# The last attention of an eight-layer kernel: its projections in pairs through a PSUM bank of their own

## The chip, the cores and the metric

The kernel runs on one core of a Trainium2 chip. The metric is the device time of one execution in microseconds; the runs shown are whole executions, and the profile is one further execution with the hardware profiler on.

## What is computed

Eight sequences of 256 tokens with 256 features pass through four layers, each an attention and a feed-forward part, both with a residual and a layer norm. All of it is in fp32. The change touches the last attention and, by one line, the mixture of experts behind it. Of the reference, what matters is this:

```python
# attention of layer 3: 16 heads of 16, 4 key heads, two score maps a = 0, 1 for each head
q, k = rope(x @ Wq), rope(x @ Wk)                       # 2 * 16 per head
scores = softmax(where(causal, NEG, q_a . k_a) / 4)     # for a = 0 and 1
lam = exp(sum(lq1 * lk1)) - exp(sum(lq2 * lk2)) + LAM_INIT
diff = softmax(where(causal, NEG, scores[0] - lam * scores[1]))
att = diff @ v
att = att * rsqrt(mean(att * att) + 1e-8) * rms_w * (1 - LAM_INIT)
x = layernorm(x + att @ Wo)
# feed-forward of layer 3: 32 experts, the 4 likeliest for each token
w, i = top_k(softmax(x @ gate), 4);  w = w / sum(w)
x = layernorm(x + sum_k w_k * down_i(up_i(x) * silu(gate_i(x))))
```

## The kernel before

The eight phases run one after the other (`attn0`, `ffn0`, ... `attn3`, `ffn3`). In `attn3` and `ffn3` the order of the instructions on PE, DVE, ACT and POOL is the order in which the program writes them; SP, which issues the DMAs, is ordered by a scheduler. [...]

`attn3` cuts a sequence into six units: two with the first 128 queries and two of four heads each (`qc` 0), and four with the last 128 queries, one head each (`qc` 1). The 48 units run as a pipeline of 51 rounds (loop at L833). In a round, for the unit n, PE multiplies queries and keys (L641) and adds the mask (L654), DVE takes four maxima (L658), ACT the exponentials with their sums (L661; 16 short ones for `qc` 0, 8 long ones for `qc` 1). For the unit n-1, `factors` (L667) prepares the ratio c on POOL, and `differences` (L686) takes the second map off the first on DVE in two halves (L695, L699), which POOL shifts and scales (L703). For n-2, `turned` (L709) transposes on PE and ACT takes the second exponential (L722). For n-3, `values` (L728) multiplies with V.

Beside this run two chains of small steps. `project(b)` (L584) makes the rotated queries and keys of the next sequence: 12 products of 128x256, each taken out of PSUM by DVE with a table (L599), and the product for V (L615, L619). The loop advances it by one step after `values` and by one or two after the first half of the differences. `finish(b)` (L748) ends a sequence. Its six steps are: (1) transpose the outputs, divide, square (L755 to L767); (2) root of the mean of squares (L770 to L789), for which ACT loads the table of Ln and then that of Exp (L779, L780) between POOL's small instructions, all in 32 columns; (3) transpose again and copy (L794, L798); (4) output product, residual, statistics (L803 to L808); (5) normalise; (6) transpose x for the next phase. The loop takes one step a round, after the first half. When sequence 3 has ended, the sort of the experts' group 0 begins as a third chain (`others`), whose last part scatters the rows by 32 indirect DMAs on POOL (L953), three a round.

PSUM has eight banks, two for each of four tags. The scores use `a` and `s`; `values` uses `o`; everything else uses `t`: the projections, `turned`, and steps 1, 3, 4 and 6 of `finish`.

`ffn3` (L2063) computes two groups of 63 tiles of 128 sorted rows. For each tile: fetch (L1959, three tiles in one DMA on SP), transpose (L1970), gate and up (L1978), Silu, transpose back (L1994), down (L2000, eight tiles later in the first group), copy to `yg` (L2008, two buffers) and store (L2010). Between the tiles of group 0, it works off what the attention left over: the last `finish`, and behind it the sort of group 1, whose scatter must have landed before group 1 is fetched:

```python
left = list(left) + [self.ffn3_sort(w, 1, act)]
for j, _ in enumerate(self.ffn3_experts(w, 0, act)):
    if len(left) > 1 and j % 3 != 2:
        continue
    while left and next(left[0], StopIteration) is StopIteration:
        left.pop(0)
```

Of the kernel before, what the change touches and what calls it, by code (L numbers as in the profile page):

```python
# [10 lines left out]
F32 = mybir.dt.float32  # L11
BF16 = mybir.dt.bfloat16
I32 = mybir.dt.int32
U32 = mybir.dt.uint32
AF = mybir.ActivationFunctionType
ALU = mybir.AluOpType
AX = mybir.AxisListType

P = 128
NB = 8  # L20
T = 256
D = 256
BLK = 512
NBLK = NB * T // BLK
LN_EPS = 1e-5
NEG = -1e30
# [5 lines left out]
TILES0 = [(n * T * 2 + 4 * (P - 1)) // P for _, n in GROUPS0]  # L32
ROW0 = P + 8
# [6 lines left out]
class Model:  # L40
# [493 lines left out]
    def attn3_load(self, pool, keep):  # L534
        wo = self.load(keep, "a3_wo", [P, 2, D])
        rms = self.load(keep, "a3_rms_w", [P, 1])
        l = pool.tile([P, 4, 256], F32, name="w_l", tag="w_l")
        for i, x in enumerate(("lq1", "lk1", "lq2", "lk2")):
            self.nc.sync.dma_start(out=l[:, i, :], in_=self.ins[f"a3_{x}"].to_broadcast([P, 256]))
        return dict(  # L540
            l=l,
            wq=self.load(pool, "a3_wq", [P, 2, 1024], split=2),
            wk=self.load(pool, "a3_wk", [P, 2, 512]),
            wv=self.load(pool, "a3_wv", [P, 2, 64]),
            wo=wo,
            tq=self.load(pool, "c_tq3", [P, 2, T]),
            ck=self.load(pool, "c_ck3", [P, 2, T]),
            sk=self.load(pool, "c_sk3", [P, 2, T]),
            rms=rms,
        )  # L550

    def attn3(self, w, act, keep, start=False, beside=None):
# [5 lines left out]
        nc = self.nc  # L558
        lam_init = 0.8 - 0.6 * math.exp(-0.3 * 0)

        e = []
        l = w["l"]
        for i in range(2):
            pr = l[:, 2 * i, :]
            nc.vector.tensor_tensor(pr, pr, l[:, 2 * i + 1, :], ALU.mult)
            sm = act.tile([P, 16], F32, tag=f"lsm{i}", name="lsm", bufs=1)
# [3 lines left out]
        nlam = act.tile([P, 4, 4], F32, tag="nlam", name="nlam", bufs=1)  # L570
        nl = nlam.rearrange("p s h -> p (s h)")
# [3 lines left out]
        wo = w["wo"]  # L575
        nc.vector.tensor_scalar(wo, wo, w["rms"], 1.0 - lam_init, ALU.mult, ALU.mult)
        Vs = []
        for i in range(2):
            V = act.tile([P, 2, 4, 32], F32, tag=f"V{i}", name=f"V{i}", bufs=1)
            nc.gpsimd.memset(V, 1.0)  # L580
            Vs.append(V)
        qTs, kTs, oT, oSs = {}, {}, {}, {}

        def project(b):  # L584

            if start:
                self.transpose_x(b)
            xT = self.xT[b // 2][:, :, (b % 2) * T : (b % 2 + 1) * T]
            qT = act.tile([P, 8, T], F32, tag="qT", name="qT")
            kT = act.tile([P, 2, T], F32, tag="kT", name="kT")  # L590

            def turn(out, wt, i, tab):
                ps = self.ps("t")[:, :T]
                for c in range(2):
                    nc.tensor.matmul(
                        ps, wt[:, c, i * P : (i + 1) * P], xT[:, c, :],
                        start=(c == 0), stop=(c == 1),
                    )
                nc.vector.tensor_tensor(out, ps, tab, ALU.mult)  # L599

            for a in range(2):
                k = kT[:, a, :]
                turn(k, w["wk"], 2 * a, w["ck"][:, a, :])
                yield
                x = act.tile([P, T], F32, tag="kh", name="kh", bufs=1)
                turn(x, w["wk"], 2 * a + 1, w["sk"][:, a, :])
                nc.gpsimd.tensor_tensor(k, k, x, ALU.add)
                yield
            for j in range(8):
                turn(qT[:, j, :], w["wq"], j, w["tq"][:, j % 2, :])  # L610
                yield
            ps = self.ps("t")[:, :128].rearrange("p (t n) -> p t n", t=2)
            for t in range(2):
                for c in range(2):
                    nc.tensor.matmul(  # L615
                        ps[:, t, :], xT[:, c, t * P : (t + 1) * P], w["wv"][:, c, :],
                        start=(c == 0), stop=(c == 1),
                    )
            nc.vector.tensor_copy(  # L619
                Vs[b % 2][:, :, :, 0:16], ps.rearrange("p t (s d) -> p t s d", s=4)  # L620
            )
            qTs[b], kTs[b] = qT, kT
            yield

        class Unit:

# [101 lines left out]
            def values(u):  # L728

                V = Vs[u.b % 2]  # L730
                if u.h0 == 0:
                    oT[u.b, u.qc] = self.ps("o").rearrange("p (h q) -> p h q", h=4)
                o = oT[u.b, u.qc]
                for c in range(1 + u.qc):
                    for s in range(4):
                        out = o[32 * s : 32 * s + 32, u.h0 : u.h0 + u.nh, :]
                        x = u.p[s] if u.qc == 0 else u.p[s][:, c : c + 1, :]
                        nc.tensor.matmul(
                            out, V[:, c, s, :], x, start=(c == 0), stop=(c == u.qc)
                        )  # L740
                if u.h0 + u.nh == 4:
                    oS = keep.tile([P, 4, P], F32, tag=f"oS{u.qc}", name="oS", bufs=1)
                    self.copy(oS, o)
                    oSs[u.b, u.qc] = oS
                    if u.qc == 1:
                        done.append(finish(u.b))
# [68 lines left out]
            yield  # L815

        others = []
        projections, ends, done = [], [], []

        def step(queue, n=1):  # L820

            while n and queue:
                if next(queue[0], StopIteration) is StopIteration:
                    queue.pop(0)
                else:
                    n -= 1

        for _ in project(0):
            pass
        units = [  # L830
            Unit(b, qc, h0) for b in range(NB) for qc in range(2) for h0 in range(0, 4, 2 - qc)
        ]
        for n in range(len(units) + 3):  # L833

            def at(back):
                return units[n - back] if 0 <= n - back < len(units) else None

            u, last = at(0), at(1)
            if u and u.qc == 0 and u.h0 == 0:
                step(projections, 100)  # L840
                if u.b + 1 < NB:
                    projections.append(project(u.b + 1))
            if last:
                last.factors()
            step(others)
            if u:
                u.scores()
            if at(3):
                at(3).values()
            step(projections)  # L850
            halves = last.differences() if last else iter(())
            next(halves, None)
            step(projections, 2 if u and u.qc == 0 else 1)
            step(ends)
            next(halves, None)
            next(halves, None)
            if not self.scattering:
                step(others, 2)
            if at(2):
                at(2).turned()  # L860
            ends += done
            done.clear()
        return ends + others
# [1199 lines left out]
    def ffn3(self, w, act, left, start=False):  # L2063

        self.down = None
        if start:
            for b in range(NB):
                self.transpose_x(b)  # L2070
            left = [self.ffn3_sort(w, 0, act)]
        if 0 not in self.sorted:
            for x in left:
                for _ in x:
                    pass
            left = []
        left = list(left) + [self.ffn3_sort(w, 1, act)]
        for j, _ in enumerate(self.ffn3_experts(w, 0, act)):

            if len(left) > 1 and j % 3 != 2:  # L2080
                continue
            while left and next(left[0], StopIteration) is StopIteration:
                left.pop(0)
        for x in left:
            for _ in x:
                pass
        put = self.ffn3_combine(0, act, 2)
        for j, _ in enumerate(self.ffn3_experts(w, 1, act)):

            if j >= 8:  # L2090
                next(put, None)
        for _ in put:
            pass
        for _ in self.ffn3_combine(1, act, 1):
            pass
# [194 lines left out]
```

## Time and profile before

| What | us |
|---|---|
| median of 3 runs | 2521.76 (2521.01 to 2522.95) |
| the profiled execution | 2531.46 |
| its span, first to last instruction | 2529.7 |
| opening projection, PE busy all the time | 1756 to 1768 |
| first scores of the attention | 1768.5 |
| attention, last differences begin | 2215.7 |
| first tile of the experts transposed | 2230.12 |
| last tile of group 0, first of group 1 | 2355.43, 2367.07 |
| combining the last outputs, to the end | 2473.9 to 2529.7 |

Over the whole span PE is busy 87%, DVE 57%, ACT 41%, POOL 36%, with a mean granted clock of 0.947 on PE. These shares are means over phases with different limits: in the attention it is DVE that has the least idle time. In the rows of the profile, a line such as L599 is the program's line, `out<-in` its tiles, and the text in brackets the idle time of the engine just before and what ended it. In the rows of waits the three numbers are the total in us, the number of times, and the longest. fp32 products show two matmul records for each instruction of the program.

### The profile page before, as it was taken

What the parts mean: (1) busy time and instruction counts of PE and PEld (TensorE: products, weight loads), DVE (VectorE), ACT (ScalarE), POOL (GpSimd) and SP (SyncE); (2) the same over time, 40 slices, a digit from 0 to 9 for tenths busy, and PEclk for the clock granted to TensorE, in tenths of its full rate; (3) what the DMA queues carried; (4) which work ended last, traced back from release to release, by engine and by line L of the source; (5) the groups of instructions that cost most, each with busy time, mean ns of one, the idle gap of its engine ahead of it and who ended that gap; (6) DMA issues with size and microseconds to landing.
All of it is one profiled execution on the core that took longest, in us unless ns stands there. A gap on an engine that the chain in (4) does not pass through costs nothing. (4 is left out here: it accounts for less than half of the span.)

```text
span 2529.7 us, 36310 instructions
## 1 busy us (share of the span) xinstructions
PE 2207.9 (87%) x12016; PEld 1497.5 (59%) x12016; DVE 1431.1 (57%) x3593; ACT 1046.2 (41%) x3005; POOL 917.4 (36%) x1725
## 2 busy tenths in 40 slices
PE   7999789899999999999999999998878777678990
PEld 4454588756666666666664465555555554467780
DVE  4555486754544544544465454565888888645363
ACT  1334355553544544534431112121766755634440
POOL 1222443343433323333312321000566647824445
PEclk9999999999999999999999999999989988789995
DMA  5000411100000100000250011002000000155663
GB/s 159 1 1 1 157 48 40 53 14 4 4 3 3 52 1 1 1 1 1 81 197 0 1 50 51 1 0 102 1 2 1 1 1 28 38 139 174 200 203 96
DMA packets 92309, 120.76 MB, mean 48 GB/s; under 512 B 9757, under 2 KB 79582, under 8 KB 91102
## 3 DMA queue, kind: packets, MB, share of 16 engines
q1 hardware_dynamic: 82270, 95.75, 11.8%
q0 software_dynamic: 8192, 21.11, 2.8%
q8 instruction: 100, 1.64, 0.3%
q10 hardware_dynamic: 1664, 1.57, 0.2%
q14 instruction: 83, 0.68, 0.1%
HBM read 67.53 MB, written 50.88 MB: 47 GB/s over the span
## 5 line engine op out<-in xcount | busy, mean ns | idle before, releaser
L1388 POOL TENSOR_SCALAR p<-p,rs 128x128 f32<-128x128 f32 (+1 forms) x256 | 104.6, 428 | 293.7 <-DVE rs L1386 289.4
L1378 ACT ACTIVATE p<-ps_s,nm,rq 128x128 f32<-128x128 f32 (+1 forms) x256 | 128.0, 507 | 151.0 <-DVE nm L1376 151.0
L1306 ACT ACTIVATE sq<-ps_a 128x512 f32<-128x512 f32 x126 | 76.0, 603 | 228.1 <-PE ps_a L1298 225.9
L146 POOL TENSOR_SCALAR rsq<-bnmv 128x2 f32<-128x2 f32 x64 | 13.6, 213 | 385.4 <-DVE bnmv L184 377.8
L661 ACT ACTIVATE e<-ps_a,nm 128x128 f32<-128x128 f32 (+1 forms) x256 | 105.9, 435 | 108.9 <-DVE nm L658 95.4
L1307 DVE TENSOR_REDUCE ssk<-sq 128x4 f32<-128x512 f32 x64 | 43.8, 686 | 172.6 <-ACT sq L1306 172.6
L703 POOL TENSOR_SCALAR v<-e,r,nmd 128x128 f32<-128x128 f32 (+1 forms) x256 | 134.9, 540 | 10.0
L1298 PE MATMUL ps_a<-w_a_wq,xT 128*128 128x512 f32 x256 | 123.2, 604 | 12.1 <-DVE k L1320 9.2
L1978 PE MATMUL ps_a<-w_f_gup,xTg 128*128 x504 | 113.1, 349 | 12.8 <-DVE xTg L1972 5.5
L720 PE MATMUL ps_t<-ident,v 128*128 128x128 f32 x384 | 67.8, 312 | 62.3 <-DVE qT L599 30.6
L1298 PE MATMUL ps_a<-w_a_wv,xT 128*128 128x512 f32 x256 | 120.5, 593 | 1.0 <-ACT q L1331 1.0
L695 DVE SCALAR_TENSOR_TENSOR e<-e,c 128x128 f32<-128x128 f32 (+1 forms) x256 | 105.6, 462 | 23.0 <-POOL c L682 22.8
L1307 DVE TENSOR_REDUCE ssq<-sq 128x4 f32<-128x512 f32 x64 | 43.9, 686 | 131.0 <-ACT sq L1306 131.0
L1298 PE MATMUL ps_a<-w_a_wk,xT 128*128 128x512 f32 x248 | 116.5, 593 | 0.0
L1426 PE MATMUL ps_o<-w_a_wo,attT 128*128 128x256 f32 x512 | 111.8, 379 | 0.0
L661 ACT ACTIVATE e<-ps_s,nm 128x128 f32<-128x128 f32 (+1 forms) x256 | 106.8, 451 | 0.0
L1426 PEld LDWEIGHTS ps_o<-w_a_wo,attT 128*128 128x128 f32 x512 | 96.7, 190 | 12.8
L1162 DVE SCALAR_TENSOR_TENSOR yg<-ps_t,xg,yg 128x128 f32<-128x128 f32 x266 | 93.1, 350 | 13.8 <-PE ps_t L1151 3.5
L1365 PE MATMUL ps_s<-kT,qT 128*128 128x256 f32 (+1 forms) x512 | 99.5, 327 | 0.0
L1978 PEld LDWEIGHTS ps_a<-w_f_gup,xTg 128*128 128x128 f32 x504 | 83.3, 199 | 25.2 <-issue 10.5
L720 PEld LDWEIGHTS ps_t<-ident,v 128*128 128x128 f32 x384 | 49.4, 160 | 81.8 <-POOL nmd L700 29.9
L1412 PE MATMUL ps_o<-pT,V 128*128 128x256 f32 x256 | 79.5, 392 | 19.3 <-ACT pT L120 19.3
(410 smaller groups left out, 6072.7 us busy)
## 6 DMA issues: line engine op xcount, KB each, us to landing
rows<-zero SPq DMA_DIRECT2D x42, 384.0 KB
xg<-rows SPq DMA_DIRECT2D x42, 384.0 KB
outs<-yg SPq DMA_DIRECT2D x42, 384.0 KB
w_f_gup<-in_f_gup SPq DMA_DIRECT2D x8, 768.0 KB
w_f_w<-in_f_w SPq DMA_DIRECT2D x8, 512.0 KB
w_f_down<-in_f_down SPq DMA_DIRECT2D x8, 384.0 KB
w_f_up<-in_f_up SPq DMA_DIRECT2D x5, 512.0 KB
lrows<-zero SPq DMA_DIRECT2D x12, 204.0 KB
```

The costliest lines, as they stand in the source:

```text
L661: nc.scalar.activation(e[:, s, j * nk : (j + 1) * nk], sc[s][:, j, :], AF.Exp, bias=nm[:, s, j : j + 1], scale=1.0, accum_out=sums[:, s, j ...
L695: nc.vector.scalar_tensor_tensor(d[:, s, h, :], u.e[:, s, h, 1, :], u.c[:, s, h : h + 1], d[:, s, h, :], ALU.mult, ALU.add,)
L703: nc.gpsimd.tensor_scalar(u.v[:, s, h, :], d[:, s, h, :], u.r[:, s, h, 0:1], nm[:, s, h : h + 1], ALU.mult, ALU.add,)
L720: nc.tensor.transpose(ps[:, s, c, :], x, self.ident)
L1162: nc.vector.scalar_tensor_tensor(acc[j], y, c, acc[j], ALU.mult, ALU.add)
L1298: nc.tensor.matmul(ps, self.xt(u.b, t, c), w[which][:, c, u.cols], start=(c == 0), stop=(c == 1),)
L1307: nc.vector.tensor_reduce(out, sq, AX.X, ALU.add)
L1365: nc.tensor.matmul(sc[:, j, :], u.qT[:, h0 + j, qc * P : (qc + 1) * P], u.kT[:, h0 + j, 0:nk], start=(j == 0), stop=False,)
L1378: nc.scalar.activation(u.p[qc][:, h0 + j, :], sc[:, j, :], AF.Exp, bias=nm[:, j : j + 1], scale=r[:, j : j + 1], accum_out=u.sums[qc][:, h ...
L1388: nc.gpsimd.tensor_scalar(u.p[qc][:, j, :], u.p[qc][:, j, :], ri[:, j : j + 1], 1.0, ALU.mult, ALU.mult,)
L1426: nc.tensor.matmul(y[:, t, :], attTs[b][:, h, t * P : (t + 1) * P], w["wo"][:, h, :], start=(h == 0), stop=(h == 15),)
L1978: nc.tensor.matmul(ps, xT[j][:, c, :], w["gup"][:, bass.ds(er[j], 1), c, :].rearrange("p o f -> p (o f)"), start=(c == 0), stop=(c == 1),)
```

## The change

`project(b)` no longer yields. It returns six pairs of a PE part and a DVE part, and a seventh for V. A pair makes two products side by side in one bank (128x512), which DVE takes out with one instruction. Keys are added on POOL with one instruction for both. One of the two `o` banks, `bank_x`, is kept for these pairs for the whole attention, and the other, `bank_o`, for `values`. In the loop, the PE part of a pair ends a round and its DVE part comes early in the next; V goes into the third round of a sequence. Before the loop, the six pairs and V of the first sequence run one after the other. `finish` gets two steps in each round.

```diff
-        qTs, kTs, oT, oSs = {}, {}, {}, {}
+        qTs, kTs, oSs = {}, {}, {}
+        bank_o, bank_x = self.ps("o"), self.ps("o")
         def project(b):
...
+            kh = act.tile([P, 2, T], F32, tag="kh", name="kh", bufs=1)
+            two = bank_x.rearrange("p (a t) -> p a t", a=2)
+            def turn(wt, *cols):
+                for a, i in enumerate(cols):
+                    for c in range(2):
+                        nc.tensor.matmul(
+                            two[:, a, :], wt[:, c, i * P : (i + 1) * P], xT[:, c, :],
+                            start=(c == 0), stop=(c == 1),
+                        )
+            def out(to, tab, add=False):
+                nc.vector.tensor_tensor(to, two, tab, ALU.mult)
+                if add:
+                    nc.gpsimd.tensor_tensor(kT, kT, kh, ALU.add)
...
+            return [
+                (partial(turn, w["wk"], 0, 2), partial(out, kT, w["ck"])),
+                (partial(turn, w["wk"], 1, 3), partial(out, kh, w["sk"], True)),
+            ] + [
+                (
+                    partial(turn, w["wq"], j, j + 1),
+                    partial(out, qT[:, j : j + 2, :], w["tq"]),
+                )
+                for j in range(0, 8, 2)
+            ], (v, v_out)
...
             def values(u):
-                if u.h0 == 0:
-                    oT[u.b, u.qc] = self.ps("o").rearrange("p (h q) -> p h q", h=4)
-                o = oT[u.b, u.qc]
+                o = bank_o.rearrange("p (h q) -> p h q", h=4)
...
-        for _ in project(0):
-            pass
+        pairs, v = project(0)
+        for f, g in pairs + [v]:
+            f()
+            g()
+        pairs = []
...
             if last:
                 last.factors()
+            if out:
+                out()
+                out = None
+            if u and n % 6 == 0 and u.b + 1 < NB:
+                pairs, v = project(u.b + 1)
             step(others)
             if u:
                 u.scores()
             if at(3):
                 at(3).values()
-            step(projections)
+            extra = v if n % 6 == 2 and pairs else None
+            if extra:
+                extra[0]()
             halves = last.differences() if last else iter(())
             next(halves, None)
-            step(projections, 2 if u and u.qc == 0 else 1)
             step(ends)
+            if extra:
+                extra[1]()
             next(halves, None)
             next(halves, None)
             if not self.scattering:
                 step(others, 2)
             if at(2):
                 at(2).turned()
+            step(ends)
+            if pairs:
+                f, out = pairs.pop(0)
+                f()
...
-            if len(left) > 1 and j % 3 != 2:
+            if len(left) > 1 and j % 3 == 0:
                 continue
```

The new file is 404 lines longer than the old one, because it holds `attn3` twice. Behind the first `attn3`, which has the lines above up to `values`, the diff puts a different `finish`, and behind that a copy of the end of `attn0` (its stores of zeros and its loop), a second `attn3_load` and a second `attn3`. The `finish` of the first one takes the root by an integer shift and three Newton steps on GpSimd:

```diff
+            nc.vector.tensor_scalar(ms, ms, 1.0 / 16.0, 1e-8, ALU.mult, ALU.add)
+            half = self.small.tile([P, 2, 16], I32, tag="half", name="half")
+            nc.vector.tensor_scalar(half, ms.bitcast(I32), 1, None, ALU.arith_shift_right)
+            rr = self.small.tile([P, 2, 16], F32, tag="rr", name="rr")
+            nc.vector.tensor_scalar(
+                rr.bitcast(I32), half, -1.0, float(0x5F3759DF), ALU.mult, ALU.add
+            )
+            yield
+            for _ in range(3):
+                t = self.small.tile([P, 2, 16], F32, tag="rt", name="rt")
+                g.tensor_tensor(t, rr, rr, ALU.mult)
+                g.tensor_tensor(t, t, ms, ALU.mult)
+                g.tensor_scalar(t, t, -0.5, 1.5, ALU.mult, ALU.add)
+                g.tensor_tensor(rr, rr, t, ALU.mult)
+                yield
```

Both definitions stand in the body of the same class, where Python keeps the later one. The second `attn3` has the loop shown above, and below its `values` the lines of `finish` as they were before, with Ln and Exp.

## The prediction

> **What bounds the kernel now.** I read the page's 40 slices first, to place the change: the last attention lies at some 1,756 to 2,227 us and the last mixture of experts behind it. Then busy times by stage, one row for each stretch between two equal points of the program (columns: length, busy time and instructions of PE, weight loads, DVE, ACT and POOL, granted clock, DMA share, GB/s):
>
> ```profile
> core 0: us, PE busy (x) PEld busy (x) DVE busy (x) ACT busy (x) POOL busy (x), PEclk, DMA share, GB/s
> 1838.41:1892.45 54.04, 42.96 (x352) 29.83 (x352) 46.03 (x104) 36.79 (x146) 33.74 (x83) 0.88 0.01 2
> 1892.45:1946.30 53.85, 43.94 (x364) 30.27 (x364) 45.17 (x102) 37.58 (x148) 32.90 (x80) 0.88 0.01 1
> 2096.65:2215.73 119.08, 85.04 (x682) 55.59 (x682) 87.46 (x195) 74.74 (x294) 94.87 (x191) 0.80 0.10 36
> 2230.12:2355.43 125.31, 106.84 (x601) 90.45 (x602) 56.46 (x195) 53.40 (x183) 45.75 (x103) 0.92 0.57 171
> ```
>
> One sequence of the attention (six rounds) takes 54 us, of which DVE works 46: DVE bounds it, with some 8 us of holes. In the third row, two sequences with the scatter of the sorted rows beside them, POOL is as loaded as DVE. In the experts PE leads. What the holes are, over 3.6 sequences (1838 to 2031; total, times, longest):
>
> ```profile
> DVE V L619 <- PE ps_t L615: 7.8, 4, 2.3
> DVE nm L658 <- PE ps_a L654: 6.9, 7, 1.9
> DVE e L695 <- POOL c L682: 6.2, 6, 1.9
> DVE res L164 <- PE ps_t L803: 5.3, 3, 1.8
> PE ps_t L720 <- DVE qT L599: 16.6, 13, 2.4
> POOL ms L781 <- ACT rr L780: 7.8, 4, 2.0
> ```
>
> So 26.2 us, 7.3 a sequence, is DVE's; PE's wait for projections to leave its transpose banks matters only as far as it comes back in the second row. DVE's rows in order of time show the holes beside the evictions:
>
> ```profile
> 2021.24 0.29 DVE L619 COPY V<-ps_t 128x128 f32<-128x128 f32 x1 [2.30 <-PE ps_t L615]
> 2022.54 1.00 DVE L695 SCALAR_TENSOR_TENSOR e<-e,c 128x256 f32<-128x256 f32 x2 [1.00 <-POOL c L682]
> ...
> 2030.62 0.41 DVE L599 TENSOR_TENSOR kh<-ps_t,w_c_sk 128x256 f32<-128x256 f32 x1
> 2030.95 0.41 DVE L599 TENSOR_TENSOR kT<-ps_t,w_c_ck 128x256 f32<-128x256 f32 x1
> 2033.12 0.69 DVE L164 TENSOR_TENSOR res<-ps_t,X 128x512 f32<-128x512 f32 x1 [1.75 <-PE ps_t L803]
> ```
>
> Last the border between the experts' two groups, on SP's queue, then its longest wait, then PE:
>
> ```profile
> 2356.82 0.36 SPq L2010 DMA_DIRECT2D outs<-yg  x1
> 2360.96 0.36 SPq L1959 DMA_DIRECT2D xg<-rows  x1
> 2361.42 0.96 SPq L2010 DMA_DIRECT2D outs<-yg  x2
> ...
> SPq L1959 <- DMA rows<-X,r_slots: 3.4, 2, 2.4
> ...
> 2366.06 1.22 PE L2000 MATMUL ps_o<-w_f_down,hT 96*128 x2 [3.44 <-ACT yg L2008]
> 2367.07 1.06 PE L1970 MATMUL ps_t<-ident,xg 128*128 128x128 f32 x4
> ```
>
> The first fetch of group 1 waits for its scatter, whose last issue is at 2358.39; two stores queue behind that fetch, so ACT gets no yg buffer and PE stands 3.44 us.
>
> **The change part by part.** First, what is executed. The new file defines attn3 twice; the later definition is the method. Its finish(b) is the old one, with Ln and Exp on ACT. The arithmetic on bits and the three Newton steps stand only in the first definition (as do its stores of zeros on SP), and never run. Live are: the paired projections with banks of their own, two finish steps a round instead of one, and the experts' rule for what is left over. I cost these three.
>
> *Evictions.* A sequence loses 12 of 128x256, which start 0.33 us apart (2030.62 to 2030.95), and gains 6 of 128x512; the nearest row, a reduction of a full bank, starts every 0.60. 3.60 for 3.96: -0.36. The matmuls are the same. The two POOL additions of 0.74 become one, between 0.74 and 1.48; I take 1.2, on an engine that is free there.
>
> *Holes inside a sequence.* I laid the six rounds out with these durations. V now follows the values in a round where ACT is not held by the Ln, so its 2.2 us goes (bounds: 0 to -2.2; nearest 0.3, what the first sequence without a finish shows). The output product comes after the aT copy has long ended: res falls from 1.5 to about 0.35. Against that, three things. Step 2 of the finish now follows step 1 in the same round and stands at its end: from L777 on POOL through Ln, table, Exp to the second L787 is 4.7 us (1962.98 to 1967.70). Queued behind it on POOL are the next round's affine selects and c (0.9), for which DVE's L695 waits; c comes 6.6 us after DVE begins that round, and DVE (eviction, four maxima, every other time a copy) is ready for it after 3.5: 3.1 us for 1.7. Behind it on ACT are the next Exps, 1.6 us late but inside that same wait. Second, DVE's eviction heads the round and waits for a pair that PE puts after transposes, output product and X transposes; behind it are the four maxima, and ACT behind those. Third, in the two rounds of a sequence with 16 short Exps (5.6 us) the loop Exps, scores 1.55, maximum 0.7 makes 7.9, against 6.9 of DVE work, once projections no longer fill it. Together these two make about 4.1 for the 1.9 of the maxima before. Sum: -2.2 - 1.2 + 1.4 + 2.2 - 0.36 = -0.2 a sequence; I say -2 us over six sequences, with +-1.5 each as my error of reading, and -1.6 for the first, which has no finish to hold it.
>
> *One bank.* The Trainium skill (Perfetto Trace Analysis, Matmuls) says that independent groups of matmuls should rotate through PSUM banks so that the eviction of one overlaps the next. The trace before does so in its opening projection: eight evictions of qT start every 0.86 us, PE never idle. By the rule each of the 48 new pairs would show its eviction: PE 8 x 0.215 = 1.72, then drain and eviction, next start after 2.62; 0.9 x 48 = 43 us on PE. By the order of the trace, 42 of the pairs have most of a round between the eviction and the next pair, and pay nothing. The rule holds for the opening six, which run one after the other: +5.4 us, all on the path, since ACT and DVE have nothing else there (bounds: 0 if the V product hid it, +7 at the lower clock of the first rows).
>
> *Table loads.* The skill (ScalarE: Activation LUTs, What ACT_TABLE_LOAD costs) prices a switch at 2.66 us with its drain. In the trace the load takes 1.28 and Ln and Exp stand 0.02 from it; by the page the chain would be 7.5 long and c 2.8 later, 17 us over six sequences. The trace decides; the page's figure serves as the slow end.
>
> *Two steps a round.* Each finish ends three rounds earlier, so the sort of group 0 starts in round 30 instead of 32, and its 32 scatters (1.3 us each on POOL, three a round) run in rounds 34 to 44 instead of 37 to 47. Their number is unchanged. Before, two Ln chains fell among them, with DVE waits of 4.75 and 6.12 where the usual round has 3.3; after, one: -2.5. The last finish but one leaves the closing rounds: its residual and statistics (2 us of DVE) and product (1.7 of PE) no longer stand before the last values at 2226.85, for whose buffers the experts' fetch waits: -2.5. Attention in sum: -2 - 1.6 - 2.5 - 2.5 + 5.4 = -3.2.
>
> *Experts.* finish(7) took steps at tiles 2, 5, 8 and so on, now at 1, 2, 4, 5, 7, 8. Its products (L803 1.9 us, L794 0.6) move into PE's 5.44 us wait for xg at 2241.6 to 2247.1: -2.5. If that cover were gone, they would cost the same as before. The sort of group 1 starts at tile 10 instead of 20, and its scatters end ten tiles sooner, some 15 us, past the beats on POOL and the outs on SP; both queues have room (46 of 125 us; SP waits for tiles). The fetch at the border then no longer waits on SP: 2360.96 becomes 2357.22 or earlier, -3.7 (bounds: 0, if SP's order delays it elsewhere, to -5.5, if it comes early enough that only the pipeline's drain is left). Sum: -6.2.
>
> Total -9.4. The profiled execution took 2531.46 us (span 2529.7 and 1.8 around it), 9.7 above the median of the runs, 0.4%; I take the difference over to the median as it is: 2521.8 - 9.4 = 2512.
>
> **The rivals.** *A wash.* The compressed finish and the loop of the short Exps give back 1 us a sequence more than I read, and SP's order keeps the fetch late: +6 +3, 2521. For it: my per-sequence sum is the small difference of large terms. *Slower.* The 4.7 us chain at the head of the fourth round holds POOL and ACT, and PE's product, pair and scores follow late into the fifth and first. If DVE's idle time passes 7.7 us a sequence (7.3 plus the 0.36 saved), the attention loses. With 2 us more in each of those, +14 to +16 over seven: 2512 + 16 = 2528. For it: ACT already waits 33 us for maxima. Against it: every step of the chain stood in some round before. *PE freed is worth more.* If the 16.6 us of PE waits were behind most of the maxima's and res waits, and no loop takes their place, 2 us a sequence more go: 2500. *The Newton steps run.* Only if I misread which definition counts. Then two table loads and two small ACT instructions a sequence (3 us) give way to some twelve POOL instructions of 0.33, split over rounds: 1.6 less wait for c, about 2502.
>
> **How the numbers follow.** My forecast 0.45 (2505 to 2519), wash 0.25 (2515 to 2526), slower 0.17 (2522 to 2536), freed PE 0.10, Newton 0.03. About 5 us, 0.2%, is what a measurement can tell from no change. Faster beyond it: 0.40 + 0.06 + 0.13 = 0.59; within: 0.05 + 0.16 + 0.01 = 0.22; slower: 0.19. The range 2499 to 2528 leaves out the worse half of the slower case and the end of the freed PE.
>
> **What would show it.** Sixteen table loads for Ln and Exp still there, and no integer shift: the finish is the old one. Evictions of 128x512, 48 of them, near 0.68 us each, in the opening 2.6 us apart. No wait of V above 0.5; DVE's wait for c once a sequence, near 3 us, in its fourth round. Sequences of 53 to 54 us. The last scatter of rows near 2340, and the hole between the groups 4 us shorter. I am wrong if a sequence moves by over 2 us either way, or if the hole stays.

## The result, and the profile after

The changed kernel takes 2552.55 us (median of 4 runs, 2550.49 to 2555.32) against 2522.02 (2521.01 to 2522.95) for the one before: a ratio of 1.012 [1.0106, 1.0134], 30.5 us slower. The profiled execution took 2555.32 (span 2553.6); that of before, 2531.46, lay 9.7 above its median, so the spans differ by 23.9 only.

The same stages as before, in the profile of the changed kernel (columns as above): two sequences, the two with the scatters, group 0 of the experts.

```profile
1845.86:1904.89 59.03, 46.93 (x359) 33.03 (x361) 44.70 (x97) 36.81 (x146) 33.53 (x81) 0.85 0.00 1
1904.89:1965.22 60.33, 46.92 (x359) 33.75 (x361) 45.17 (x97) 37.05 (x147) 33.53 (x81) 0.84 0.00 1
2138.32:2254.55 116.23, 88.14 (x667) 60.31 (x669) 85.54 (x186) 73.31 (x293) 90.15 (x185) 0.78 0.08 29
2267.47:2387.48 120.01, 105.02 (x601) 89.06 (x602) 56.61 (x195) 53.61 (x185) 48.15 (x105) 0.94 0.63 192
```

A sequence takes 59 to 60 us instead of 54. DVE works a little less than before, 44.9 instead of 45.7, as the larger evictions promised; its holes went from 8.1 to 14.6 us (means over three sequences). PE does the same matmuls and is busy 3 to 4 us longer in these two, at a granted clock of 0.85 instead of 0.88 (over three sequences 0.84 instead of 0.91). Added up by the trace, the first scores come 5.2 us later (1768.5, 1773.75), the end of the last values 37.4 later (2226.8, 2264.2), and the experts take 13.5 less.

DVE's holes over 3.6 sequences (1846 to 2060), then PE's over the same stretch (total, times, longest):

```profile
DVE qT L988 <- PE ps_o L982: 22.2, 12, 2.9
DVE nm L1052 <- PE ps_a L1048: 11.0, 15, 1.2
DVE res L164 <- PE ps_t L1195: 6.6, 4, 2.6
DVE r L1065 <- ACT e L1055: 4.5, 6, 1.0
DVE nm L1052 <- remote: 3.6, 4, 1.4
DVE e L1089 <- POOL c L1076: 3.1, 4, 1.1
```

```profile
PE ps_t L154 <- ACT p L1116: 12.5, 4, 3.1
PE ps_t L1114 <- DVE att L1152: 11.5, 4, 2.9
PE ps_t L1114 <- ACT aT L1190: 6.5, 4, 1.9
```

The wait for V is gone from the list. In its place stands the eviction at the head of the round (L988), which waits for the pair's matmuls (L982), 6.2 us a sequence; the maxima behind it (L1052) wait longer too. PE is late for three waits of its own, all in the steps of `finish` and `turned` that stand ahead of the pair. PE's rows in order of time show what happens behind such a wait:

```profile
1952.07 1.89 PE L982 MATMUL ps_o<-xT,w_a_wk 128*128 128x256 f32 x8
...
1960.83 1.91 PE L1114 MATMUL ps_t<-ident,v 128*128 128x128 f32 x8
1963.56 3.78 PE L982 MATMUL ps_o<-xT,w_a_wq 128*128 128x256 f32 x8 [0.81 <-DVE V L1003]
...
1974.04 1.25 PE L1114 MATMUL ps_t<-ident,v 128*128 128x128 f32 x8 [2.88 <-DVE att L1152]
1975.12 3.37 PE L982 MATMUL ps_o<-xT,w_a_wq 128*128 128x256 f32 x8
```

The eight matmuls of a pair take 1.89 us in one round and 3.78 in the next: exactly twice. The granted clock (the third column from the right) is the reason. In the trace it has only two values, 1.00 and 0.50, and all 90 stretches between its changes are whole multiples of 3.41 us. So here are PE's rows in stretches of 3.41 us, laid where the clock can change:

```profile
1954.90:1958.31 3.41, 2.45 (x24) 1.44 (x28) 2.29 (x6) 2.58 (x12) 3.31 (x8) 1.00 0.00 0
1958.31:1961.73 3.42, 3.42 (x29) 3.04 (x22) 3.42 (x6) 3.01 (x13) 3.26 (x7) 0.50 0.00 0
1961.73:1965.14 3.41, 2.60 (x9) 1.93 (x8) 3.34 (x11) 2.20 (x7) 1.65 (x4) 0.50 0.00 0
1965.14:1968.55 3.41, 3.41 (x18) 2.34 (x20) 0.96 (x3) 0.00 (x0) 3.23 (x11) 0.50 0.02 5
1968.55:1971.97 3.42, 2.60 (x28) 1.39 (x24) 2.70 (x5) 1.91 (x9) 0.41 (x2) 1.00 0.00 0
1971.97:1975.38 3.41, 1.34 (x10) 1.15 (x11) 3.31 (x9) 2.44 (x10) 1.93 (x4) 1.00 0.00 0
1975.38:1978.79 3.41, 3.41 (x12) 2.32 (x14) 2.09 (x6) 2.37 (x4) 2.35 (x6) 0.50 0.00 0
```

PE stood idle from 1971 to 1974 at the full clock, and was put to half at 1975.38, 1.3 us after it had begun to work again, when the stretch with the gap (1.34 of 3.41 us busy) had ended. So the bill for a wait is paid by what comes after it, and here that is the pair, with the scores of the next round behind it. Of the 18 pairs in the three sequences from 1845.86 on, nine are slow, eight of them with 3.29 us or more and one with 2.83; together they take 14.0 us more than at full speed. (In e9, the same kernel once more, it is seven pairs and 11.6 us.)

### The profile page after: what moved, and what is told of

The parts are those of the page before. It is cut to its first block, busy times and chain, and to the rows that moved or that the text cites. A ratio compares the mean times of both kernels' runs of the same rounds, so it can differ in the third digit from the quotient of the medians.

```text
span 2553.6 us, 36252 instructions
## 1 busy us (share of the span) xinstructions
PE 2229.7 (87%) x11961; PEld 1524.7 (60%) x12016; DVE 1423.8 (56%) x3545; ACT 1044.3 (41%) x3005; POOL 917.5 (36%) x1717
## 3 DMA queue, kind: packets, MB, share of 16 engines
q1 hardware_dynamic: 82270, 95.75, 11.6%
q8 instruction: 101, 1.65, 0.3%
## 5 line engine op out<-in xcount | busy, mean ns | idle before, releaser
L1097 POOL TENSOR_SCALAR v<-e,r,nmd 128x128 f32<-128x128 f32 (+1 forms) x256 | 136.5, 544 | 10.1
L154 PE MATMUL ps_t<-ident,X 128*128 128x128 f32 x256 | 46.2, 312 | 69.2 <-DVE X L190 34.9
L1089 DVE SCALAR_TENSOR_TENSOR e<-e,c 128x128 f32<-128x128 f32 (+1 forms) x256 | 98.8, 437 | 10.8 <-POOL c L1076 10.8
L982 PE MATMUL ps_o<-xT,w_a_wq 128*128 128x256 f32 x256 | 91.4, 521 | 9.2 <-DVE V L1003 6.0
## 6 DMA issues: line engine op xcount, KB each, us to landing
w_f_down<-in_f_down SPq DMA_DIRECT2D x8, 384.0 KB, 10.6
```

Source lines behind the costliest of these rows:

```text
L982: nc.tensor.matmul(two[:, a, :], wt[:, c, i * P : (i + 1) * P], xT[:, c, :], start=(c == 0), stop=(c == 1),)
L1089: nc.vector.scalar_tensor_tensor(d[:, s, h, :], u.e[:, s, h, 1, :], u.c[:, s, h : h + 1], d[:, s, h, :], ALU.mult, ALU.add,)
L1097: nc.gpsimd.tensor_scalar(u.v[:, s, h, :], d[:, s, h, :], u.r[:, s, h, 0:1], nm[:, s, h : h + 1], ALU.mult, ALU.add,)
```

## The experiments

Four theories. *Half clock*: PE's waits at the end of the round halve its clock, and the pair behind them is on the path at half speed. *Place*: the pair stands on the path before the scores, whatever its speed. *Two steps*: the second finish step a round crowds the round. *One bank*: evicting the pair at the head of the round is the cost. The experiments' kernels leave out the definition that never runs, so their line numbers differ. The runs fall into four groups (e1 to e4, e5 to e8, e9 to e12, e13 to e16). The kernel before, run in each, took 2532, 2531, 2521 and 2523 us, so ratios to it are compared; 0.1% is 2.5 us. "Three sequences" is the time between the reciprocals (DVE's r, one for each unit) of the 9th and the 27th unit, where the kernel before has 161.4 us and the changed one 178.4; the last two columns belong to this stretch. "Filler" is work added for PE alone, whose result is written over.

| Run | ratio, 95% interval | three sequences, us | PE busy, us | clock |
|---|---|---|---|---|
| the change, again (e9) | 1.012 [1.0104, 1.0137] | 178.6 | 137.0 | 0.85 |
| one finish step (e2) | 1.004 [1.0026, 1.0054] | 165.4 | 136.5 | 0.85 |
| filler in the gap (e3) | 1.001 [1.0001, 1.0019] | 164.6 | 146.3 | 0.99 |
| pair early (e4) | 1.0001 [0.9991, 1.001] | 165.5 | 131.3 | 0.91 |
| filler at the end (e5) | 1.0312 [1.0288, 1.0335] | 195.5 | 157.8 | 0.92 |
| pair early, V late (e6) | 0.9991 [0.9983, 1.0] | 166.5 | 137.0 | 0.87 |
| e6 with filler (e7) | 0.997 [0.9963, 0.9978] | 158.1 | 145.4 | 1.00 |
| e7, two banks at first (e10) | 0.9932 [0.9916, 0.9949] | 159.6 | 146.0 | 0.99 |
| e10, half the filler (e12) | 0.997 [0.9958, 0.9983] | 163.8 | 139.4 | 0.94 |
| e10, no filler (e13) | 0.9937 [0.992, 0.9953] | 163.0 | 128.3 | 0.91 |
| e10, twice the filler (e14) | 1.0052 [1.0035, 1.0068] | 176.6 | 170.3 | 1.00 |

### More work for PE, in the gap and behind it

In e3, nothing is moved: the pair is issued once more behind the values.

```diff
             if at(3):
                 at(3).values()
+            if pairs:
+                pairs[0][0]()
```

> The changed kernel with each pair's eight matmuls issued one time more, right behind the values' product, into the same bank; the pair at the end of the round writes over them, so this is only added work for TensorE (some 1.9 us a round) in a stretch where it has nothing to do. Theory 'half clock': the idle stretch is cut, the pairs at the end of the round take 1.9 instead of 3.4 to 3.8 us, a sequence falls by about 5 us, total 2520 to 2530 us. Theory 'place of the pair' alone: the pairs stay where they are and as long as they are, 2552 us, or up to 10 us more where the added work delays the turned tiles. Theory 'two steps': no change, 2552 us.

It came out at 1.001: with 1.9 us *more* work a round, 28 of the 30 us are gone. The rows of the pair's matmuls over three sequences (duration in ns, lowest, median, highest), first of the changed kernel, then of e3:

```profile
L982 PE MATMUL ps_o<-xT,w_a_wq x101: 378/633/794, 1844.8 to 2024.9; 128*128 128x256 f32 x101
```

```profile
L601 PE MATMUL ps_o<-xT,w_a_wq x194: 379/379/483, 1841.0 to 2005.7; 128*128 128x256 f32 x194
```

The queries' pairs fall from a median of 633 ns to 379, and the pairs are where they were. That is what half clock asked for, and place alone and two steps exclude. The counter-check puts the same added work at the end of the round, behind the gap:

```diff
             if pairs:
                 f, out = pairs.pop(0)
                 f()
+                f()
```

> The changed kernel with each pair's eight matmuls issued twice at their own place at the end of the round; the second writes over the first. The same added work as in the filler of before, but it does not cut the idle stretch in front of the pair, and stands on the path before the scores. Theory 'half clock' (it is the stretch without work in front of the pair that counts): each of the 42 pairs adds 1.9 us (the second at full speed) to 3.6 us to the path, less where DVE has other work then; a sequence goes from 59.5 to some 65 to 72 us, or at best stays if the longer work keeps the scores at full speed. Total 2560 to 2630 us on the scale on which the changed kernel has 2552. Theory 'any added work keeps the clock up, wherever it stands': 2535 to 2550 us.

1.0312, three sequences 195.5 us: 17 more than the changed kernel for 18 more pairs of 1.89 us. So the same work behind the gap, on the path, does not help: the clock rises from 0.85 to 0.92, and the kernel still loses half of the added time.

### The pair moved

```diff
             if at(3):
                 at(3).values()
             extra = v if n % 6 == 2 and pairs else None
             if extra:
                 extra[0]()
+            elif pairs:
+                f, out = pairs.pop(0)
+                f()
...
-            if pairs:
+            if extra:
                 f, out = pairs.pop(0)
                 f()
```

> The changed kernel with the pair's eight matmuls moved from the end of the round to right behind the values' product (in the one round of six in which V uses the bank, at the end as before). The bank is empty there since the head of the round. Theories 'place of the pair' and 'half clock': the pair leaves the path before the scores in five of six rounds, a sequence falls from 59.5 to 54 or 55 us, total 2518 to 2526 us, and the gaps that DVE has before the maxima shrink. Theory 'two steps': 2545 us or more. Theory 'one bank' (the pair's eviction at the head of the round is what costs): 2550 us.

1.0001. Three sequences take 165.5 us, 0.9 more than with the filler: taking the pair off the path and making it run at full speed on the path are worth the same. So the loss is neither place alone nor clock alone, but the slow pair in that place. One bank alone is excluded, since the bank and the eviction were not touched. In e6, the pair of V's round is early as well; it is taken out in the middle of the round, and V's matmuls come last:

```diff
-            extra = v if n % 6 == 2 and pairs else None
-            if extra:
-                extra[0]()
+            vee = n % 6 == 2 and pairs
+            if pairs:
+                f, out = pairs.pop(0)
+                f()
...
-            if extra:
-                extra[1]()
+            if vee:
+                out()
...
-            if pairs:
-                f, out = pairs.pop(0)
-                f()
+            if vee:
+                v[0]()
+                out = v[1]
```

> The changed kernel with every pair right behind the values' product; in the one round with V that pair is taken out of the bank in the middle of the round, V's four short matmuls stand at the end, and V is taken out at the next round's head. So no pair is left at the end of a round. The pair early alone gave 1.0001 of the time before, with one pair of six still at the end of a round (1.96 us of DVE's waits a sequence). Theories 'place' and 'half clock': another 1 to 2 us for each of seven sequences, ratio 0.994 to 0.997. If V's round was not on the path: 1.000.

0.9991, and 1.0 us more for three sequences than e4: the gain is a third of the least that I expected, and not established. e7 issues each of these early pairs twice (a second `f()` behind the first).

> The kernel with every pair early and V late, and each pair's eight matmuls issued twice there (the second writes over the first), 1.9 us more work for TensorE a round, off the path. Theory 'half clock': the turned tiles and the scores run at full speed more often, another 1 to 3 us for each sequence on top of the kernel without the filler, ratio 0.990 to 0.995. Theory 'place' alone: no better than without the filler, or up to 1 us a round slower where the added work delays the finish steps' transposes: 0.995 to 1.010.

Three sequences take 158.1 us at a clock of 1.00, 8.4 less than e6, as half clock asked for. The whole gained less than the forecast, 0.997: the sequences behind these three hardly changed.

### One finish step a round

```diff
             if at(2):
                 at(2).turned()
-            step(ends)
             if pairs:
```

> The changed kernel with one finish step a round instead of two (the step at the end of the round taken out). Theory 'two steps' (the second step's transposes, output product and residual crowd the end of the round and make the 30 us): a sequence falls from 59.5 to about 54.5 us, total 2522 us. Theory 'place of the pair' (the pair's eight matmuls stand at the end of the round, behind waits of TensorE and right before the scores) and theory 'half clock' (after such a wait they run at half speed): the turned tiles still wait for the attention's first step and for the probabilities, so at most the wait for the copy of the attention (1.4 us a sequence) goes, and the ends come later: 2545 to 2556 us.

1.004, between the two forecasts: I had expected nearly nothing from the waits that go, and 13 of 17 us over three sequences went. The mean clock stayed at 0.85, but of 18 pairs only four ran slowly instead of nine, and their extra time fell from 14.0 to 6.0 us: without the second step the half-speed stretches fall mostly on other work. What the other 5 of the 13 us were is not taken apart. So the mean clock of a stretch says little; what stands on the path when it is low decides. Where the pair is early and doubled, the same step taken out of the loop gives the opposite (e11, from e10):

> The same with one finish step a round (the step at the end of the round taken out), where the half speed has been cured. Theory 'the second step only hurt by the waits that halved the clock' : no gain in a sequence (52 to 53 us either way), and the last sequence's ends come two or three rounds later, so the last tiles and the tail are 2 to 5 us later: 0.1 to 0.2% slower than with two steps. Theory 'two steps crowd the round whatever the clock': 1 to 2 us gained in each of six sequences, 0.3 to 0.5% faster than with two steps.

0.997 [0.996, 0.9981] against 0.9932 with two steps. Beside a filled gap the second step is worth some 9 us. Three sequences take 166.7 us at a clock of 0.95 instead of 159.6 at 0.99, so a part of this can be the clock again; but a gain from a less crowded round does not show.

### The opening

From e7, with a second bank for the first sequence:

```diff
-            two = bank_x.rearrange("p (a t) -> p a t", a=2)
+            spare = [bank_x, bank_o] if b == 0 else [bank_x]
...
-        for f, g in pairs + [v]:
-            f()
-            g()
+        opening = pairs + [v]
+        opening[0][0]()
+        for i, (_, g) in enumerate(opening):
+            if i + 1 < len(opening):
+                opening[i + 1][0]()
+            g()
```

> Every pair early with its second issue, V late (0.997), and in the opening, where the values' bank is still empty, the six pairs of the first sequence take turns in the two banks, each issued before the pair ahead of it is taken out. The prediction put the single bank at +5.4 us for the opening alone, the traces at +5.2. Theory 'one bank costs the opening': 4 to 6 us less than with one bank, ratio 0.9945 to 0.9955. If the opening waits for something else (half speed of its first pairs, the tables): 0 to 2 us less, 0.996 to 0.997.

0.9932, 17 us faster than the kernel before and 9 to 10 less than e7: twice the forecast. PE in the opening, of the changed kernel and of e10:

```profile
1755.25 3.78 PE L982 MATMUL ps_o<-xT,w_a_wk 128*128 128x256 f32 x8 [0.98 <-DVE kT L988]
1759.82 3.78 PE L982 MATMUL ps_o<-xT,w_a_wq 128*128 128x256 f32 x8 [0.78 <-DVE kh L988]
1764.39 1.99 PE L982 MATMUL ps_o<-xT,w_a_wq 128*128 128x256 f32 x8 [0.78 <-DVE qT L988]
```

```profile
1754.61 7.17 PE L604 MATMUL ps_o<-xT,w_a_wq 128*128 128x256 f32 x32 [1.23 <-DVE kT L610]
```

With one bank the pairs wait 0.78 us or more for the eviction ahead of them, and two of them ran at half speed (3.78 us). With two banks four pairs run in one piece, at full speed. The forecast had the waits only. The first scores start at 1762.6, instead of 1773.8 in the changed kernel and 1768.5 in the one before.

### How much added work

e12 issues only the first four of each early pair's matmuls twice, e13 none, e14 all of them three times.

> The kernel with two banks in the opening, and half of the added work: of each pair only the first four matmuls are issued twice (0.95 us a round instead of 1.9). Theory 'half clock, set by how busy TensorE has been over some microseconds': half of the work keeps the clock up in a part of the rounds only, a sequence between 52.7 us (full filler) and 55.5 us (none), so 0.1 to 0.5% slower than with the full filler. If the added work's place alone counts, or if the clock was up already: as fast as with the full filler or 0.1% faster.

> Every pair early, V late, two banks in the opening, and no added work. Half of the added work gave 54.4 to 55.0 us a sequence and 0.997, all of it 52.5 to 54.7 and 0.9932. Theory 'half clock, set by how busy TensorE is': 55 to 56.5 us a sequence, ratio 0.997 to 1.000. Theory 'place' (the added work does nothing by itself): 0.992 to 0.994.

> The same with each pair issued three times (3.8 us of added work a round). Theory 'half clock': with the added 1.9 us every pair but one ran at full speed already, so more can bring nothing there, and in the rounds with the attention's first step its transposes come up to 1.9 us later; ratio 0.993 to 0.998, a sequence 52.5 to 55 us. Theory 'the more work the better': under 0.992.

No dose curve came of it. Three sequences take 163.0, 163.8, 159.6 and 176.6 us for none, half, all and twice, and the totals 0.9937, 0.997, 0.9932 and 1.0052. With the pair off the path and two banks, none does as well as all within the intervals, against my forecast (with one bank, e7 was 0.2% ahead of e6); too much is slower, with PE busy 170 of 177 us. That half, from another group, is slower than none stays unexplained; what the clock is worth once the pair stands early is not settled by these runs.

### The experts' rule, and the kernel before with more work

e1 and e16 are the kernel before with nothing but `j % 3 == 0`; e15 is the kernel before itself.

> The kernel before with nothing but the experts' new rule for the leftover steps (every third tile instead of two of three). The prediction put the whole experts' stage at -6.2 us, of which -3.7 at the border of the two groups. The traces of before and after put the experts at -13.5 (group 0 -5.3, border -3.9, group 1 -4.3). If all of that is the rule's: 2508 to 2511 us. If the gains inside the groups came with the later start that the changed attention leaves: 2518 us. If the rule is worth nothing alone: 2522 us.

> The kernel before with the experts' new rule alone, which measured 0.9977 (-5.8 us) in the first call. If the rule's worth depends on the chip's memory and not on the attention ahead of it: on a chip where the stage of the changed kernels takes 285 to 287 us, 0.994 to 0.995 (-13 us); on one where it takes 293 to 297, 0.9977 again. If the rule alone is worth -6 and the rest came with the changed attention: 0.9977 on either.

> The kernel before, unchanged, for its profile on the chip of this call: 1.000, 53.5 to 54.0 us a sequence, and from the first expert tile to the end 299 us if its stage is the kernel's own, 303 to 308 if the chip of the second call was slower there.

0.9977 [0.997, 0.9985] and 0.9975 [0.9965, 0.9985]: the rule is worth 6 us in both groups. The kernel before itself (e15) comes out at 0.9996 [0.9986, 1.0007], with 53.6 us a sequence. In this fourth group, the stage from the first expert tile's transposition to the end takes 290.5 us in the kernel before, which neither forecast had, and 286.0 with the rule. In the first profile of the kernel before it was 299.6, in an execution 9.7 us above the median; so some 9 of the 13.5 us were never a gain of the change. It also means that the attention lost some 36 us (30.5 + 6), as the 37.4 of the last values says. The same stage of e9:

> The changed kernel once more, without the definition that never runs, beside the other kernels of this study. It should be 1.010 to 1.014 of the kernel before. What is open is its experts' stage: from the first expert tile to the end it took 285 us in its first profile, where every other kernel with the new rule takes 293 to 297 and the kernel before 299. If the short stage belongs to this kernel's order of work it comes back at 284 to 287; if it was the chip or the moment, it is at 293 to 297 here.

287.9 us and 1.012: the changed kernel repeats in full. What is left of the differences in this stage lies between the groups: 294 to 298 us in the first two with the same code, of which 97 to 101 from the first to the last tile of group 1, where the later two have 92 to 94. Its cause stays open. Last, the rule with each projection of the kernel before doubled (`for c in (0, 1, 0, 1)`):

> The kernel before with the experts' new rule (0.9977 alone), and each of the 12 projections of a sequence with its two matmuls issued twice into the same bank, some 0.5 us more work for TensorE a projection, the second writing over the first. The trace of before has its projections at a mean of 401 ns a matmul where a pair at full speed has 236, so TensorE runs at half speed there too. Theory 'half clock also sets the pace before': a sequence gains 0.5 to 2 us, ratio 0.993 to 0.997. Otherwise the added work is hidden or delays the evictions: 0.998 to 1.005.

1.0061 [1.0043, 1.0079], against 0.9977 without: 21 us slower. The first reciprocal comes 10 us later (in the opening, PE has no room), and three sequences take 162.9 at a clock of 0.98 instead of 161.3 at 0.91. In the kernel before half speed was there too, and lifting it in this way brought nothing. It fell on other work than the projections: their matmuls have a median of 379 ns there, which is full speed. (The 401 ns of the expectation are the length of a record, the 236 the distance of two.)

## Why the prediction was wrong

The forecast was 2512, in a range from 2499 to 2528, and faster than before; it is 2552.6 and slower. One term of the sum carries the miss.

*What failed: the eviction that heads the round.* In "Holes inside a sequence" the second and third points gave 4.1 us a sequence for the 1.9 of the maxima before, +2.2. It measured 22.2 us for qT and 16.1 for nm (the rows above, and 1.5 of one not shown) over 3.6 sequences: 10.6 a sequence, +8.7. I saw that the eviction waits for a pair behind transposes, output product and X transposes, but costed that pair with the 1.9 us of full speed, and "42 of the pairs ... pay nothing". What those waits do to the pair behind them was missing. DVE's holes over three sequences of e3, where the same pairs stand in the same place at full speed, show it:

```profile
DVE nm L671 <- PE ps_a L667: 11.1, 18, 0.7
DVE e L708 <- POOL c L695: 7.0, 3, 2.7
DVE r L684 <- ACT e L674: 4.5, 6, 1.0
DVE qT L607 <- PE ps_o L601: 3.5, 6, 1.2
DVE res L164 <- PE ps_t L814: 1.7, 1, 1.7
```

qT and nm are 14.6 us there, 4.9 a sequence; with r, DVE's wait for the short Exps of the third point, it is 6.4. In the changed kernel all three make 12.0 a sequence over the same stretch. So of the 7.9 us above the forecast of 4.1, about 5.6 went with the half speed, and 2.3 were missing at full speed, too. The granted clock stands in the prediction's first table, 0.88 and 0.80 in stages where the whole span has 0.947, and no term was drawn from it.

The Trainium skill (TensorE: Matmul & The Clock Gate, Part 1: The HAM clock gate) states the rule: the array's clock is halved after an idle window of about 3.4 us and restored after a busy one. The 11.6 to 14.0 us that the slow pairs lose in three sequences are 3.9 to 4.7 a sequence; seven sequences make, as an estimate, 27 to 33 of the 36 of the attention. The trace agrees on the length of the windows: half speed lasts from 1958.3 to 1968.6 and from 1975.4 to 1978.8, three stretches of 3.41 us and one. It differs on the cause. The stretch with the gap of 2.88 us was 39% busy, and the one before 1958.3, with no gap over 0.7 us, was 72% busy. Here the measurement decides: a window need not be empty.

*The rival that came nearest* was the slower one, in the right place (PE's pair and scores late, DVE idle above 7.7 us a sequence) but with a wrong cause and 2 us a sequence where it was 6.

*The other terms of a sequence.* V's wait of 2.2 went, as said. c was to cost 3.1 us once a sequence, and cost 0.8, because DVE now comes to it late; with the new wait gone it comes out as laid out, 8.9 us in three sequences of e10. res was to fall to 0.35 and stayed at 1.65 each time; in e3 it is 1.7 in three sequences. The sum itself has a slip: six times -0.2 is -1, not -2. The evictions gave what they should: 0.68 us each, and 44.9 us of DVE work a sequence for 45.7. With the pair cured, three sequences take 1.8 us less than before with the added work (e10) and 1.6 more without (e13): -0.6 and +0.5 a sequence, where I said -0.2.

*One bank.* 42 pairs that pay nothing for the bank, and +5.4 for the opening: +5.2 in the trace, with 2.78 us from pair to pair for the 2.62 that I worked out. That the number fits is in part luck: two pairs at half speed (3.8 us) are inside it, and the first pair starts 6.7 us earlier than the first projection before (1747.9, 1754.6). That it could be had for nothing was in sight, since the values' bank is empty then: e10 starts its first scores 6.0 us ahead of the kernel before.

*Two steps a round.* The scatters of group 0 moved as laid out but began 9 us later by the clock (2106.8 for 2097.8), because the sequences ahead were longer. From the reciprocal of the 45th unit to the end of the last values it is 37.1 us instead of 41.5: -4.4 for the -2.5 of the tail. Whether the other -2.5 was there under the loss stays open: the three sequences from the 27th to the 45th unit, 185.5 us before and 202.8 in the changed kernel, take 181.6 in e10, but 186.0 in e13 without the added work.

*Experts.* -6.2 forecast, -5.8 and -6.3 measured alone. At the border the last tile of group 0 and the first of group 1 are 7.7 us apart instead of 11.6: -3.9 for -3.7. The fetch still waits for the scatter, but the stores behind it no longer starve PE:

```profile
SPq L2363 <- DMA rows<-X,r_slots: 2.5, 2, 2.1
```

```profile
2392.80 2.63 PE L2404 MATMUL ps_o<-w_f_down,hT 96*128 x8 [0.36 <-ACT yg L2412]
2395.27 0.60 PE L2374 MATMUL ps_t<-ident,xg 128*128 128x128 f32 x4
```

The wait of 3.44 us for yg is 0.36. *Dead code and tables*: the 16 table loads for Ln and Exp are there, 1.28 us each; the Newton steps never ran.

## What to carry to other kernels

A matmul is costed by its place: before it is put at the end of a round, ask what PE waited for in the 3 or 4 us ahead of it. Where PE stood idle for more than half of them, as before 1975.4, cost it at double; where for nearly a third, as before 1958.3, it can happen (9 of 73 stretches that were 60 to 80% busy). When such a group is late, first move it into the stretch where PE is idle (e4): that recovered as much as added work in the gap did. A stage's granted clock below that of the span is a question to be asked of the trace row by row, and whether the slow stretch is on the path is the second one: e2 had the same mean clock as the slow kernel.

## What the runs showed of the hardware

Adding 1.9 us of matmuls to each round made the kernel 28 us faster, with the clock up from 0.85 to 0.99. The clock fell after the gap and not in it: 1.00 while PE stood idle, 0.50 from about 1.3 us after it went on, because it changes only on a grid of 3.41 us (so it does in e2, e3 and the kernel before).

Counted over the whole execution of the changed kernel, on this grid and by the matmul records of the trace: of the stretches at 1.00, all 26 in which PE was busy for less than 40% were followed by one at 0.50, 9 of 73 with 60 to 80%, and none of 519 with 80% or more. Of those at 0.50, none of 22 under 80% was followed by full speed, and 44 of 58 with 80% or more were. So half speed comes after little work and leaves only after much. The 10 us above fit this but for one: the stretch from 1961.7 was 76% busy, the one from 1965.1 brought full speed back, and why the one from 1958.3, busy throughout, did not stays open, as for the other 13 of its kind.
